# Layer 0's expert tiles and the scan's preparation rearranged: results leave from another queue, fetched rows are transposed behind a later tile, one logarithm for each preparation

## Chip, core and metric

The kernel runs on one core of one Trainium2 chip. The metric is device time in microseconds of one execution. Four runs of the kernel before gave 4164.61, 4164.91, 4173.64 and 4187.34, a median of 4169.28. One further execution was profiled.

## What is computed

Four images of 256 channels and 32 by 32 pixels go through two layers. All of it is float32.

- Layer 0, mixer: attention with 8 heads in which each row keeps only its largest scores, a 3 by 3 convolution of the values, a projection, and a residual.
- Layer 0, feed-forward: each of 4096 pixels is normalised and routed to 2 of 8 experts. An expert is `gelu(t @ w1 + b1) @ w2 + b2` with 256 hidden units, and the weighted sum and the residual give the pixel's new value.
- Layer 1, mixer: `x` is normalised, and a selective scan is run over the pixels in four directions. Its step size is `delta = softplus(xm @ W_delta + b_delta)`, and its input is `delta * xm` times a row of B.
- Layer 1, feed-forward: again 2 of 8 experts, with 1024 hidden units.

The part of the reference that matters here, shortened:

```python
out = tokens                                   # layer 0's feed-forward
for e in range(E):
    h = jax.nn.gelu(tokens @ w1[e] + b1[e], approximate=False)
    out = out + combine[:, e:e + 1] * (h @ w2[e] + b2[e])
...
delta = jax.nn.softplus(x @ W_delta + b_delta)  # layer 1's mixer
dBx = (delta * x)[..., None] * Bm[:, :, None, :]
y = jnp.einsum('blcn,bln->blc', h, Cm) + x * D
```

## The kernel before

The images stay in SBUF in the four tiles `x[b]`, channels on partitions, 1024 pixels in the free dimension (`L`), in two halves of 512 (`HALF`).

**Routing.** For each image, pixels are normalised (`norm`), routed (`route`) and scattered as rows into expert blocks in DRAM, `slots_x0` (lines 1487 to 1503). The blocks are then worked off in tiles of `T` = 256 rows. 36 tiles (`USUAL`) are always run; three more lie in a branch that this input does not take. The order of tiles has three phases, so that image 0's rows are all in the first 15 tiles (`FIRST`) and image 1's in the first 23 (`SECOND`).

**One tile** (`tile0`, lines 1507 to 1550). SyncE (SP) loads a block's rows `xs` (259 KB, 4 buffers), and the expert's `w1` and `w2` (256 KB each, 3 buffers). VectorE (DVE) picks the biases and the rows' weights. TensorE (PE) transposes the rows into `tp`, DVE copies them to `xe`, PE makes `hp`, ScalarE (ACT) applies Gelu to `hid`, PE makes `yp`, DVE and ACT add the bias and weigh it (`ys`, 4 buffers), and SP stores `ys` into `slots_y0` (line 1550).

**Beside the tiles.** `whole(b)` (line 1565) brings an image's rows back: 16 indirect DMAs on GpSimd (POOL) fetch rows of `slots_y0` into `y` (`fetched`, line 1451; the second eight add to the first eight), and `completed` (lines 1459 to 1468) transposes them on PE and adds them to `x[b]`. After image 0 comes `Prep(0).steps`, the preparation for the scan of image 0. In the loop over tiles (lines 1573 to 1578) four steps of each generator go ahead of a tile. With `times` = 2 and `pause(8)`, the transposes come four tiles after the first fetch in program order.

This part is not written as a fixed order. A scheduler at compile time orders each engine's instructions by its own model of their times, with program order as priority, so an instruction that the model takes for ready can go ahead of earlier code. On the chip each engine, and each engine's DMA queue, then works in that order: an instruction that has to wait holds up all behind it.

Every store into `slots_y0` and every fetch from it has an address known only at run time, so a fetch waits for all earlier stores, and a store for all earlier fetches.

**The preparation** (`Prep.steps`, line 1332) is run four times. `Prep(0)` is run beside layer 0's tiles, the other three inside the scan. After the normalisation it handles `zp`, the step size before softplus, in four parts, 2 channel tiles by 2 halves, each 128 by 512. In the version before, two parts form a group `c`:

```python
yield from begin(0)          # PE zp; ACT Relu, Abs, Exp
yield from begin(1)
lost(0); lost(1)             # six DVE operations together, line 1417
nc.scalar.activation(sp[:, 2:], sp[:, 2:], AF.Ln)          # line 1430, once per group
nc.vector.scalar_tensor_tensor(dd, sp[:, h], -0.5, dd, ALU.mult, ALU.add)  # 1434
nc.gpsimd.tensor_tensor(dd, dd, sp[:, 2 + h], ALU.add)     # line 1435
```

and `rest` (line 1390) then multiplies `dx = delta * xm` on POOL (line 1393) and updates `x` on DVE (line 1394).

**The scan** (lines 1715 to 1795) is 128 turns in an order written out by hand. A turn has on DVE the scans of lines 1671, 1680 and 1697 and two products (line 1707); on PE five groups of four matmul records of 512 columns; on POOL the product `uu` (line 1658), the product of line 1691 and a small difference; and on ACT three exponentials and a copy. Twice in each turn one step of the preparation of the next image is slipped in, once at the turn's beginning and once just ahead of the scan of line 1697. Images 2 and 3 are fetched and completed in the first 32 turns, and from the second image on the pixels of the image before are routed for layer 1.

Of the kernel before, what the change touches and what calls it, by code (L numbers as in the profile page):

```python
# [11 lines left out]
F32 = mybir.dt.float32  # L12
# [4 lines left out]
AF = mybir.ActivationFunctionType  # L17
# [44 lines left out]
def metaformer(ctx: ExitStack, tc: tile.TileContext, t: dict, out: bass.AP):  # L62
# [1259 lines left out]
    class Prep:  # L1322
# [9 lines left out]
        def steps(self, room, psum, tag):  # L1332
# [44 lines left out]
            bc = room("sp", [4 * HALF])[: 2 * NS, :L]  # L1377
# [12 lines left out]
            def rest(c):  # L1390
                for h in range(NHALF):
                    cols = ts(h, HALF)
                    nc.gpsimd.tensor_tensor(self.dx[:, c, cols], self.delta[:, c, cols], xm[:, c, cols], ALU.mult)
                    nc.vector.scalar_tensor_tensor(x[b][:, c, cols], xm[:, c, cols], dsk[:, c : c + 1],
                                                   x[b][:, c, cols], ALU.mult, ALU.add)
                    yield
                    yield

            behind = iter(())
            for c in range(CT):  # L1400
                sp = room("sp", [4 * HALF]).rearrange("p (k n) -> p k n", k=4)

                def begin(h):
                    cols = ts(h, HALF)
                    zp = psum.tile([P, HALF], F32, tag=tag, name="zp")
                    for k in range(CT):
                        nc.tensor.matmul(zp, wd[:, k, ts(c, P)], xm[:, k, cols],
                                         start=(k == 0), stop=(k == CT - 1))
                    next(behind, None)
                    yield  # L1410
                    nc.scalar.activation(self.delta[:, c, cols], zp, AF.Relu, bias=bd[:, c : c + 1])
                    nc.scalar.activation(sp[:, h], zp, AF.Abs, bias=bd[:, c : c + 1])
                    nc.scalar.activation(sp[:, h], sp[:, h], AF.Exp, scale=-1.0)
                    next(behind, None)
                    yield

                def lost(h):
                    v, up, dd = sp[:, h], sp[:, 2 + h], self.dx[:, c, ts(h, HALF)]
                    nc.vector.tensor_scalar(up, v, 1.0, None, ALU.add)
                    nc.vector.scalar_tensor_tensor(dd, up, 1.0, v, ALU.subtract, ALU.subtract, reverse1=True)  # L1420
                    nc.vector.scalar_tensor_tensor(v, v, 2.0, dd, ALU.subtract, ALU.mult)

                yield from begin(0)
                yield from begin(1)
                for _ in behind:
                    pass
                lost(0)
                lost(1)
                yield
                nc.scalar.activation(sp[:, 2:], sp[:, 2:], AF.Ln)  # L1430
                yield
                for h in range(NHALF):
                    dd = self.delta[:, c, ts(h, HALF)]
                    nc.vector.scalar_tensor_tensor(dd, sp[:, h], -0.5, dd, ALU.mult, ALU.add)
                    nc.gpsimd.tensor_tensor(dd, dd, sp[:, 2 + h], ALU.add)
                yield
                yield
                behind = rest(c)
            for _ in behind:
                yield  # L1440
            yield
            yield
# [15 lines left out]

    def completed(b, h, y, psum, tag):

        for c in range(CT):
            op = psum.tile([P, HALF], F32, tag=tag, name="op")
            for i in range(4):
                nc.tensor.transpose(op[:, ts(i, P)], y[:, i, ts(c, P)], ident)
            yield
            xs = x[b][:, c, ts(h, HALF)]
            nc.vector.tensor_tensor(xs, op, xs, ALU.add)
            yield
# [5 lines left out]
    with ExitStack() as st:  # L1474
        wp = st.enter_context(tc.tile_pool(name="m0_w", bufs=1))
        pb = st.enter_context(tc.tile_pool(name="m0_b", bufs=2))
# [3 lines left out]

        b1 = load(wp, "b1_0", [P, E, CT])
        b2 = wp.tile([P, E, C], F32, tag="b2_0", name="b2_0")
        nc.sync.dma_start(b2, t["b2_0"].rearrange("e d -> (e d)").partition_broadcast(P).rearrange(
            "p (e d) -> p e d", e=E))
        tokens = [wp.tile([P, NT, W0], F32, tag=f"tok{b}", name=f"tok{b}") for b in range(B)]
        scattered = nc.alloc_semaphore("scattered")
        for b in range(B):
            d = pb.tile([P, CT, L], F32, tag="d", name="d")
            here = slot0[:, :, ts(b, NT)]
            for _ in norm(b, 0, tokens[b], pb, ps_n, "t", "t", d):  # L1490
                pass
            for _ in route(b, 0, tokens[b], here, wp.tile([P, 2560], F32, tag="numbers", name="numbers"), ps_n, "t"):
                pass

            with tc.tile_critical(name=f"scatter{b}", no_gpsimd_drain=True):
                for n in range(NT):
                    for k in range(2):
                        nc.gpsimd.indirect_dma_start(
                            out=slots_x0, out_offset=bass.IndirectOffsetOnAxis(ap=here[:, k, n : n + 1], axis=0),
                            in_=tokens[b][:, n], in_offset=None).then_inc(scattered, 16)  # L1500
                nc.gpsimd.wait_ge(scattered, 16 * 2 * NT * (b + 1))
                if b == B - 1:
                    nc.clear_and_free_semaphores([scattered])

        blocks_x, blocks_y = (a.rearrange("(k a p) c -> k p a c", a=T // P, p=P) for a in (slots_x0, slots_y0))

        def tile0(i):
            def register(k, most, engines):
                return nc.values_load(every.which[0:1, k, i : i + 1], engines=engines, min_val=0, max_val=most,
                                      skip_runtime_bounds_check_because="the minimum with that of a count")  # L1510

            block = register(1, E * BLOCKS, [mybir.EngineType.SP])
            xs = pb.tile([P, T // P, W0], F32, tag="xs", name="xs", bufs=4)
            nc.sync.dma_start(xs, blocks_x[bass.ds(block, 1)].rearrange("o p a c -> p (o a) c"))
            e = register(0, E - 1, [mybir.EngineType.SP, mybir.EngineType.DVE])
            w1 = pb.tile([P, CT, C], F32, tag="w1", name="w1", bufs=3)
            nc.sync.dma_start(w1, t["w1_0"][bass.ds(e, 1)].rearrange("o (c p) f -> p (o c) f", p=P))
            w2 = pb.tile([P, CT, C], F32, tag="w2", name="w2", bufs=3)
            nc.sync.dma_start(w2, t["w2_0"][bass.ds(e, 1)].rearrange("o (c p) f -> p (o c) f", p=P))
            b1e = pb.tile([P, CT], F32, tag="b1e", name="b1e")  # L1520
            nc.vector.tensor_copy(b1e, b1[:, bass.ds(e, 1)].rearrange("p o c -> p (o c)"))
            b2e = pb.tile([P, C], F32, tag="b2e", name="b2e")
            nc.vector.tensor_copy(b2e, b2[:, bass.ds(e, 1)].rearrange("p o d -> p (o d)"))
            best = pb.tile([P, T // P], F32, tag="best", name="best")
            nc.vector.tensor_scalar(best, xs[:, :, C], every.expert[:, i : i + 1], None, ALU.is_equal)
            wt = pb.tile([P, T // P], F32, tag="wt", name="wt")
            nc.vector.tensor_tensor(wt, best, xs[:, :, C + 1], ALU.mult)
            nc.vector.tensor_tensor(wt, wt, xs[:, :, C + 2], ALU.add)
            tp = ps1.tile([P, CT, T], F32, tag="tp", name="tp")
            for a in range(T // P):  # L1530
                for c in range(CT):
                    nc.tensor.transpose(tp[:, c, ts(a, P)], xs[:, a, ts(c, P)], ident)
            xe = pb.tile([P, CT, T], F32, tag="xe", name="xe")
            nc.vector.tensor_copy(xe, tp)
            hp = ps_h.tile([P, CT, T], F32, tag="hp", name="hp")
            hid = pb.tile([P, CT, T], F32, tag="hid", name="hid")
            for f in range(CT):
                for c in range(CT):
                    nc.tensor.matmul(hp[:, f], w1[:, c, ts(f, P)], xe[:, c], start=(c == 0), stop=(c == CT - 1))
                nc.scalar.activation(hid[:, f], hp[:, f], AF.Gelu, bias=b1e[:, f : f + 1])  # L1540
            yp = ps1.tile([P, T // P, C], F32, tag="yp", name="yp")
            for a in range(T // P):
                for f in range(CT):
                    nc.tensor.matmul(yp[:, a], hid[:, f, ts(a, P)], w2[:, f, :], start=(f == 0), stop=(f == CT - 1))
# [468 lines left out]
```

## Time and profile before

| what | value |
|---|---|
| median of 4 runs | 4169.28 us |
| the profiled execution, its own time | 4186.96 us |
| its span, first to last instruction | 4185.2 us |
| attention, to the last projection | about 0 to 1925 us |
| routing of layer 0 | 1931 to 2072 us |
| layer 0's tiles, first transpose to last `yp` | 2074.7 to 2298.3 us |
| the scan with three preparations | 2302.8 to 3597 us |
| layer 1's tiles and the output | 3597 to 4185 us |
| busy in the scan (1294 us): PE, DVE, ACT, POOL | 1227, 1162, 885, 729 us |

The profiled execution lies at the upper end of the four runs, 17.7 us over their median; 1.8 us of its time lie outside its span. In the timeline a row gives start, duration, engine, line and operation, and in brackets how long the engine was idle before, and what ended that. "SPq" is the moment at which SP issues a DMA. PE records of one line are merged, and a fast record of 512 columns takes a quarter of 1.72 us.

### The profile page before, as it was taken

What the parts mean: (1) busy time and instruction counts of PE and PEld (TensorE: products, weight loads), DVE (VectorE), ACT (ScalarE), POOL (GpSimd) and SP (SyncE); (2) the same over time, 40 slices, a digit from 0 to 9 for tenths busy, and PEclk for the clock granted to TensorE, in tenths of its full rate; (3) what the DMA queues carried; (4) which work ended last, traced back from release to release, by engine and by line L of the source; (5) the groups of instructions that cost most, each with busy time, mean ns of one, the idle gap of its engine ahead of it and who ended that gap; (6) DMA issues with size and microseconds to landing.
All of it is one profiled execution on the core that took longest, in us unless ns stands there. A gap on an engine that the chain in (4) does not pass through costs nothing. (4 is left out here: it accounts for less than half of the span.)

```text
span 4185.2 us, 50303 instructions
## 1 busy us (share of the span) xinstructions
PE 3545.5 (85%) x17502; PEld 1966.5 (47%) x17502; DVE 3040.4 (73%) x5327; ACT 2847.3 (68%) x3823; POOL 1824.1 (44%) x1436
## 2 busy tenths in 40 slices
PE   8378878888888878965387899999999999999996
PEld 5144434444444434433265334443443434688885
DVE  2689898989898989893356889889899899411112
ACT  2889999999999999973235677767667677422222
POOL 0145444554455445552413666446446546221111
PEclk8568887788778877877699999999999999999997
DMA  9300093007200000001375433323333334555565
GB/s 285 93 1 1 1 246 93 1 1 262 73 1 1 11 1 1 11 1 35 104 207 154 129 109 131 105 100 113 116 97 120 115 102 135 178 186 189 186 193 185
DMA packets 280988, 426.40 MB, mean 102 GB/s; under 512 B 31889, under 2 KB 223634, under 8 KB 280594
## 3 DMA queue, kind: packets, MB, share of 16 engines
q1 hardware_dynamic: 259920, 382.66, 30.1%
q0 software_dynamic: 17024, 38.98, 3.0%
q8 instruction: 143, 2.34, 0.2%
q10 hardware_dynamic: 3778, 1.41, 0.1%
q14 instruction: 123, 1.01, 0.1%
HBM read 280.34 MB, written 142.64 MB: 101 GB/s over the span
## 5 line engine op out<-in xcount | busy, mean ns | idle before, releaser
L490 POOL TENSOR_SCALAR dr<-s_n,last 128x1024 bf16<-128x1024 f32 x256 | 732.3, 2878 | 877.0 <-DVE state L518 343.9
L406 ACT ACTIVATE junk_a<-s_n,state 128x1024 int8<-128x1024 f32 x448 | 514.7, 1149 | 28.0 <-DVE state L524 8.0
L1691 POOL TENSOR_TENSOR da_c<-prod,come 128x1024 f32<-128x1024 f32 x128 | 248.2, 1939 | 386.3 <-DVE h L1697 381.6
L410 DVE TENSOR_SCALAR_CACHE_REDUCE junk_v<-s_n,state 128x1024 int8<-128x1024 f32 x320 | 408.7, 1277 | 8.8
L1861 ACT ACTIVATE hid<-hp,b 128x256 f32<-128x256 f32 x288 | 133.7, 474 | 355.7 <-PE hp L1859 355.1
L457 DVE SCALAR_TENSOR_TENSOR w<-s_n,win 128x1024 f32<-128x1024 f32 x256 | 350.3, 1368 | 5.3
L460 DVE MAX8 win<-w 128x8 f32<-128x1024 f32 x256 | 314.5, 1228 | 8.9
L558 ACT ACTIVATE ex<-sT 128x1024 f32<-128x1024 f32 x256 | 247.1, 1015 | 100.5 <-PE sT L550 100.3
L1658 POOL TENSOR_TENSOR uu<-dx,bb 128x1024 f32<-128x1024 f32 x128 | 305.0, 2383 | 1.4 <-DMA bb<-bc_d 1.4
L1697 DVE TENSOR_TENSOR_SCAN h<-da_c,uu 128x1024 f32<-128x1024 f32 x128 | 302.8, 2365 | 0.0
L406 ACT ACTIVATE junk_a<-s_n,guess 128x1024 int8<-128x1024 f32 x256 | 294.2, 1149 | 7.4
L1671 DVE TENSOR_TENSOR_SCAN h<-da,uu 128x1024 f32<-128x1024 f32 x128 | 290.7, 2271 | 4.6 <-POOL uu L1658 4.6
L1680 DVE TENSOR_TENSOR_SCAN h<-da,uu 128x1024 f32<-128x1024 f32 x128 | 289.8, 2264 | 0.0
L568 PE MATMUL o_ps<-ex,vT 128*32 128x256 f32 x2048 | 244.2, 454 | 46.0 <-ACT ex L558 37.1
L1701 PE MATMUL hp<-h,ident 128*128 128x512 f32 x512 | 249.3, 610 | 31.1 <-DVE h L1697 30.5
L1645 ACT ACTIVATE da_c<-delta,a_log 128x1024 f32<-128x1024 f32 x128 | 268.4, 2097 | 0.2
L1859 PE MATMUL hp<-xe,w 128*128 128x256 f32 x1152 | 259.6, 382 | 6.1 <-DVE xe L1847 5.9
L440 ACT COPY s_n<-sp 128x1024 f32<-128x1024 f32 x256 | 245.6, 1004 | 25.3 <-POOL dr L490 12.8
L1666 PE MATMUL hp<-da_c,ident 128*128 128x512 f32 x512 | 246.4, 604 | 18.3 <-POOL da_c L1691 16.3
L1870 DVE TENSOR_TENSOR ys<-yp,b2e 128x512 f32<-128x512 f32 x36 | 24.9, 692 | 325.5 <-PE yp L1867 300.3
L1666 PE MATMUL hp<-h,twice 128*128 128x512 f32 x512 | 243.8, 599 | 17.7 <-issue 13.8
L1659 ACT COPY uu<-uu 128x1024 f32<-128x1024 f32 x128 | 253.6, 1981 | 3.8 <-POOL uu L1658 3.8
(542 smaller groups left out, 7564.2 us busy)
## 6 DMA issues: line engine op xcount, KB each, us to landing
bb<-bc_d SPq DMA_DIRECT2D x128, 512.0 KB
cb<-bc_d SPq DMA_DIRECT2D x128, 512.0 KB
w<-in_w SPq DMA_DIRECT2D x36, 1024.0 KB
w2e<-in_w SPq DMA_DIRECT2D x36, 1024.0 KB
slots_x<-zeros SPq DMA_DIRECT2D x1, 33411.0 KB
slots_x<-zeros SPq DMA_DIRECT2D x1, 33282.0 KB
slots_y<-zeros SPq DMA_DIRECT2D x1, 33024.0 KB
w<-in_w SPq DMA_DIRECT2D x72, 256.0 KB
```

The source lines that it names most:

```text
L406: nc.scalar.activation(junk, self.row(r), AF.Sign, bias=thr, scale=-1.0, accum_out=u)
L410: nc.vector.tensor_scalar(junk, self.row(r), thr, None, ALU.is_lt, ALU.add, accum_out=u)
L457: nc.vector.scalar_tensor_tensor(w, self.row(r), self.win[:, r, 0:1], self.row(r), ALU.is_gt if r < LAST_DVE else ALU.is_ge, ALU.subtract, ...
L460: nc.vector.max(out=self.win[:, r, 1:], in_=w)
L490: ins = nc.gpsimd.tensor_scalar(dr, self.row(r), self.last[:, r : r + 1], None, ALU.is_lt)
L1645: nc.scalar.activation(grid(self.da_c), cols_flipped(self.prep.delta[:, self.c]), AF.Exp, scale=self.decay)
L1658: nc.gpsimd.tensor_tensor(self.uu[:, 0], self.prep.dx[:, self.c], self.bb, ALU.mult)
L1666: nc.tensor.matmul(self.hp[h], ident if eye is None else eye, view[:, ts(h, HW // NHALF), :], start=first, stop=last)
L1671: nc.vector.tensor_tensor_scan(rows.rearrange("p r w -> p (r w)"), self.da, self.uu[:, 0], 0.0, ALU.mult, ALU.add)
L1680: nc.vector.tensor_tensor_scan(hs[:, ::-1], self.da[:, ::-1], self.uu[:, 0][:, ::-1], 0.0, ALU.mult, ALU.add)
L1697: nc.vector.tensor_tensor_scan(hs, self.da_c, self.uu[:, 1], 0.0, ALU.mult, ALU.add)
L1859: nc.tensor.matmul(hp[:, f % 2], self.w1[:, c, ts(f, P)], self.xe[:, c], start=(c == 0), stop=(c == CT - 1))
```

## The change

It is confined to `Prep.steps`, `completed` and the block of layer 0's feed-forward.

- A tile becomes a class with steps. The store into `slots_y0` is issued from POOL's queue; `xs` has 6 buffers, `w1` and `w2` 4, `ys` 8. The routing gets pools of its own, which are closed before the tiles' pools are opened.
- The steps beside the tiles come after a tile, four fetches are issued in a step, and the pause is 20 steps.
- The first transpose of each group of `completed` gets an edge to the last matmul of the tile before it in program order, so the scheduler can't put it earlier. It is an order on PE alone and no semaphore. In the scan the edge is not made.
- The preparation calculates one logarithm over all four parts, `Ln(v + 1)`, after the last of them. The correction for what `v + 1` loses is two DVE operations for each part, put one part behind. The additions and `dx` are on DVE; POOL has no part in them.

```diff
-                def lost(h):
-                    v, up, dd = sp[:, h], sp[:, 2 + h], self.dx[:, c, ts(h, HALF)]
-                    nc.vector.tensor_scalar(up, v, 1.0, None, ALU.add)
-                    nc.vector.scalar_tensor_tensor(dd, up, 1.0, v, ALU.subtract, ALU.subtract, reverse1=True)
-                    nc.vector.scalar_tensor_tensor(v, v, 2.0, dd, ALU.subtract, ALU.mult)
...
+            def lost(c, cols):
+                back = self.dx[:, c, cols]
+                nc.vector.tensor_scalar(back, v[:, c, cols], 1.0, 1.0, ALU.add, ALU.subtract)
+                nc.vector.tensor_tensor(back, v[:, c, cols], back, ALU.subtract)
+
+            for i, (c, cols) in enumerate(parts):
...
+                if i:
+                    lost(*parts[i - 1])
                 yield
...
+            lost(*parts[-1])
+            yield
+            nc.scalar.activation(v, v, AF.Ln, bias=1.0)
+            yield
+            for c, cols in parts:
+                dx = self.dx[:, c, cols]
+                nc.vector.tensor_tensor(dx, dx, v[:, c, cols], ALU.add)
+                nc.vector.tensor_tensor(self.delta[:, c, cols], self.delta[:, c, cols], dx, ALU.add)
                 yield
                 yield
+                nc.vector.tensor_tensor(dx, self.delta[:, c, cols], xm[:, c, cols], ALU.mult)
+                nc.vector.scalar_tensor_tensor(x[b][:, c, cols], xm[:, c, cols], dsk[:, c : c + 1],
+                                               x[b][:, c, cols], ALU.mult, ALU.add)
                 yield
+                yield
...
+    anchor = [None]
...
+                ins = nc.tensor.transpose(op[:, ts(i, P)], y[:, i, ts(c, P)], ident)
+                if i == 0 and anchor[0] is not None:
+                    tc.add_manual_dep(ins.ins, anchor[0].ins.name,
+                                      mybir.DependencyInfo(mybir.DependencyClass.NoSync,
+                                                           mybir.DependencyReason.DATA))
...
+            def store(self):
+                for a in range(T // P):
+                    nc.scalar.mul(self.ys[:, a], self.ys[:, a], self.wt[:, a : a + 1])
+                    nc.vector.scalar_tensor_tensor(self.ys[:, a], self.xs[:, a, :C], self.best[:, a : a + 1],
+                                                   self.ys[:, a], ALU.mult, ALU.add)
+                block = self.register(1, E * BLOCKS, [mybir.EngineType.Pool])
+                nc.gpsimd.dma_start(blocks_y[bass.ds(block, 1)].rearrange("o p a c -> p (o a) c"), self.ys)
...
-            yield from fetched(b, y, range(NHALF), 2)
-            yield from pause(8)
+            yield from fetched(b, y, range(NHALF), 4)
+            yield from pause(20)
...
         for i in range(USUAL):
+            one_tile = Tile0(i)
+            for step in ("load", "small", "turned", "hidden", "result", "store"):
+                getattr(one_tile, step)()
+            anchor[0] = one_tile.last
             for first_tile, steps in beside:
                 if i >= first_tile:
                     for _ in range(4):
                         next(steps, None)
-            tile0(i)
```

## The prediction

> **What bounds the kernel now.** I read the stages first (busy time by stretch), then the timelines of the two stages that the change touches, one engine at a time. The chain of waits reaches back only to 3587 us, so it does not judge them. In layer 0's tiles PE is the bound as long as nothing interrupts it: from tile to tile `ys` (line 1546) starts 4.34 us apart (2151.04, 2155.38), with PE 80.1 of 85.4 us busy up to 2160. Then this comes, in PE's timeline:
>
> ```profile
> 2169.11 1.06 PE L1539 MATMUL hp<-xe,w 128*128 128x256 f32 x2
> 2173.87 0.56 PE L1464 MATMUL op<-ident,y 128*128 128x128 f32 x2 [3.71 <-DMA y<-slots_y,slot]
> ...
> 2229.12 1.03 PE L1539 MATMUL hp<-xe,w 128*128 128x256 f32 x4
> 2233.37 0.33 PE L1464 MATMUL op<-ident,y 128*128 128x128 f32 x1 [3.22 <-DMA y<-slots_y,slot]
> ```
>
> PE, in order, stands at transposes of rows that have not been fetched, once for each image. And in SP's and POOL's timelines:
>
> ```profile
> 2157.82 0.37 SPq L1514 DMA_DIRECT2D xs<-slots_x  x1
> 2165.41 0.40 SPq L1550 DMA_DIRECT2D slots_y<-ys  x1
> ...
> 2228.88 0.37 SPq L1517 DMA_DIRECT2D w<-in_w  x1
> 2246.47 0.40 SPq L1550 DMA_DIRECT2D slots_y<-ys  x1
> ```
>
> ```profile
> 2162.28 0.95 POOL L1451 DMA_INDIRECT y<-slots_y,slot  x1 [0.30 <-issue]
> ...
> 2168.35 1.60 POOL L1451 DMA_INDIRECT y<-slots_y,slot  x1 [5.13 <-DMA slots_y<-ys]
> ```
>
> SP is silent for 7.6 and 17.6 us: a store waits for fetches, and the loads of the next tiles are queued behind it.
>
> In the scan a turn (from one start of line 1671 on DVE to the next) takes 7.87 us where DVE is the bound and 8.58 us where PE is; with a `zp` on PE it is 10.3 (1.72 more). DVE and POOL around the preparation:
>
> ```profile
> 2848.08 1.27 DVE L1434 SCALAR_TENSOR_TENSOR delta<-sp,delta 128x512 f32<-128x512 f32 x2
> 2848.90 4.79 POOL L1435 TENSOR_TENSOR delta<-delta,sp 128x512 f32<-128x512 f32 x2 [0.40 <-DVE delta L1434]
> 2849.26 3.37 DVE L1697 TENSOR_TENSOR_SCAN h<-da_c,uu 128x1024 f32<-128x1024 f32 x1
> ...
> 2859.09 3.64 DVE L1697 TENSOR_TENSOR_SCAN h<-da_c,uu 128x1024 f32<-128x1024 f32 x1
> 2859.30 1.28 POOL L1393 TENSOR_TENSOR dx<-delta,xm 128x512 f32<-128x512 f32 x1
> ```
>
> The scan of line 1697, 2.27 us elsewhere, takes 3.37 and 3.64 beside POOL's products. POOL's help costs DVE as much as it saves.
>
> **The tiles, step by step.** From the first transpose (2074.67) to the last `yp` (2298.25) 223.6 us pass. Tile 14's `yp` ends at 2146.7; the stage before that I leave as it is. Behind it lie 21 tiles x 4.34 = 91.1 us of PE, eight groups of fetched transposes x 0.43 = 3.5, and `Prep(0)`: mean 3.4, variance 3.4, `ln_rb` 1.8, `bp` 3.4, `zp` 6.9, together 18.9 (records at full clock in the scan: 1.72 for four of 512 columns, 1.70 for 16 variance records). That is 113.5 us, so 2260.2 without a stall; 38 us are lost now. What stays lost:
>
> - *First fetch.* It comes behind tile 15's store. `yp` ends at 2151.0; 2.4 to the store (2146.7 to 2149.13), 4.1 to the fetch (2149.13 to 2153.22), 0.5 for POOL's issue (line 1941, the same 256 KB, 0.54 us). First fetch at 2158.0; eight x 1.26, the gap of 5.1, eight x 1.84 give 2187.9; 2.4 to landing. The first half's rows are in at 2183.0, the second's at 2190.3. The first half's transposes stand behind tile 21 (2177.0): a wait of 6, then 0.9 of them and a tile, and 2 more. **8 us.** Four fetches a step and the pause of 20 do that; without the edge the scheduler would put them early, as now.
> - *Second fetch.* From tile 23's end 7.0 + 10.1 + 5.1 + 14.7 + 2.4 = 39.3 us. Until tile 29's end PE has 26.0 of tiles and 18.9 of preparation, 44.9. **0**, with that work as its cover; were the preparation's matmuls done earlier, 13.
> - *POOL's power (line 1359)* lies in program order behind the second image's 16 fetches (before, ahead of them). If the scheduler puts it ahead of them it costs 0; behind eight, the 10.1 us of their issue come late against the 6 that PE has before `ln_rb`: 4 to 5; behind all 16, about 29. I take **3**.
> - *ACT.* Each part needs Relu, Abs, Exp (about 1.8) and two table loads of 1.28; 12 loads now become about 10. Three tiles with four parts and the logarithm (2.1 + 2.6) make about 27 us of ACT against 22 of PE. With the waits for Gelu **8**; bounds 4 (PE's loss from 2252.6 to 2272.9, four tiles: 3) and 14.
> - *Last tile,* 3.1 idle ahead of 2293.83 behind table loads: unchanged, **3**.
>
> The sum: 2260.2 + 22 = 2282 against 2298: **16 us less**; bounds 0 and 34. The store's queue: 36 x 0.54 us on a POOL that is idle from 2069.9 to 2153; register loads and the wait come on top, and 4.3 us a tile are there for them. Behind the waiting store on POOL stand only later stores, fetches and the power; eight `ys` hold eight tiles, 35 us, as long as the fetches' 32. SP's order loses the waiting store, and six `xs` let loads run ahead.
>
> A rule against this: the Trainium skill, "DMA: Bandwidth & Descriptors", section "Issuing engines are not separate DMA queues", says that issuing from several engines saves only the sequencer's issue time. By it alone the move would be worth an estimated 36 x 0.4 us of SP, which is idle, so nothing; the rows show why it isn't the whole: what is saved is a wait in SP's order, 7.6 and 17.6 us. "SBUF — State Buffer", section "SBUF: two separate sides", says that VectorE's fast copies keep GpSimd from writing descriptors. The row nearest to that, the fetches of 0.95 us beside `b2e` copies of 0.29, shows no such hold.
>
> **The preparation in the scan, three times.** DVE's work for a part goes from 0.34 + 3 x 0.60 + 0.65 = 2.8 us (net of overlap, lines 1419, 1420, 1421, 1434, 1394) to 0.34 + 4 x 0.60 + 0.65 = 3.4. No float32 `tensor_tensor` with both inputs in SBUF is in the trace at this size; bounds are 0.34 (line 1419) and 0.65 (line 1394), and I take 0.60, as the two-input rows beside it. So DVE gets 2.4 us more for each preparation; POOL loses 4 x (2.4 + 1.28) us. For the second preparation, 13 turns from 2811.0 to 2939.5 take 128.5 us now: among them 13.9 and 11.8 (six `lost` operations in one turn, 3.6 us; PE idle behind them) and five of 10.1 to 10.3 in which line 1697 or 1686 is stretched by POOL. After: a `lost` of 0.95 falls in each `zp` turn, where DVE has 10.3 - 7.87 = 2.4 to spare, and then eight turns have 1.2 more on DVE. 7.9 + 10.6 + 3 x 10.3 + 8 x 9.1 = 122.2: **6 us less**. The third likewise (the same turns, 128.6). The first, with fetches and completions beside it, has the same two heavy turns (14.5, 11.9) and more stretched ones: **9**. The logarithm of 2048 columns with its loads is 4.7 us of ACT in one turn, which has some 3 idle; its results are used a turn later, so 0, or 2 if that slack is not there. Sum **22 us less**; bounds 8 and 32.
>
> **Together** 38 us: 4186.96 - 38 = 4149 for the profiled execution. The median lies 17.7 lower; the four runs spread by 0.5%, with the profiled one at their upper end, and I carry the difference over: 4169.3 - 38 = **4131**.
>
> **Rivals.**
> 1. *The power or the fetches still hold PE.* The power behind all 16 fetches adds 26 us, and the tiles gain nothing: 4169 - 22 + 10 = 4157; with the edge useless, 4147. For it: program order. Against: POOL waits for tile 23's store, then 5.1 us between the two eights, and the power is ready about then.
> 2. *The scan gains nothing* because PE is the bound in those turns. Then only the tiles' 16 count: 4153. For it: PE 1227 of 1294 us busy, DVE 1162. Against: PE's idle of 1.5 us behind the heavy turns (line 1701 waits for line 1697).
> 3. *Slower.* The moved DVE operations read two SBUF tensors, as line 1697 does; if POOL's `uu` or line 1691 runs beside them, each is held by 1.4 us (3.64 against 2.27). 3 x 16 such operations x 1.4 = 67 us: 4169 - 16 - 22 + 67 = 4198. It outweighs the gain once 27 of the 48 are hit. Against: between line 1686 and 1697, where they stand, POOL has finished `uu` (2910.0 against 2910.5) and only issues an indirect DMA.
> 4. *Neither part does what it says* (waits only change place): 4169.
>
> **Numbers.** The forecast has 0.60 (4131, or somewhat less where fetches are faster); rival 1 0.17, half of it still faster by over 0.5%; rival 2 0.10; rival 3 0.06; rival 4 0.07. 0.5%, 21 us, is about what a measurement of this kernel can tell from no change. Faster 0.60 + 0.09 = 0.69, rounded up to 0.70 for the case between rivals 1 and 2; same 0.24; slower 0.06. The range: with both gains at their best 34 + 32, 4103; a little inside that, and up to rivals 1 and 2: 4108 to 4158.
>
> **What would show it.** In the tiles' stage: SP without silences of over 5 us; line 1464 waiting some 8 us for the first image and under 3 for the second; the last `yp` some 16 us sooner after the first transpose. If line 1371 or 1363 waits for line 1359, rival 1 is at work. In the scan: no turn over 11 us in the `zp` part, line 1697 at 2.27 throughout, the scan some 22 us shorter. If `tensor_tensor` rows of the preparation last over 1.2 us, rival 3. The prediction is wrong if PE's loss behind ACT's table loads grows past 14 us, or if the stores land so late from POOL's queue that the transposes wait over 20 us.

## The result and the profile after

The changed kernel takes 4165.28 us (median of 52 runs) against 4173.05 us for the kernel before (78 runs taken with them): a ratio of **0.9985, 95% interval 0.9975 to 0.9994**. By the ratio that is some 6 us less, by the medians 7.8, where 38 were forecast. The time lies above the range on record (4108 to 4158).

The stages, read off the timelines, in us. The columns are the profile before, the profile after, a second profile of the changed kernel (the run `after_again` below), and the best kernel of the experiments (`stores_lag_again`).

| stage | before | after | after, 2nd | best |
|---|---|---|---|---|
| start to the end of attention | 1924.2 | 1902.4 | 1910.5 | 1905.2 |
| to layer 0's first transpose | 150.5 | 155.9 | 139.0 | 137.7 |
| **tiles**: first transpose to last `yp` | **223.6** | **238.7** | **231.9** | **196.7** |
| to the first scan | 11.4 | 12.9 | 13.7 | 19.9 |
| **scan**: first start to last end | **1275.6** | **1259.5** | **1258.6** | **1258.8** |
| to the end of the span | 599.9 | 596.5 | 596.0 | 596.8 |

The two profiled spans differ by 19.3 us (4185.2 and 4165.9), but attention, which the change doesn't touch, differs by 21.8: spans can't be compared here, stages can. The scan got 16 us shorter, of a forecast 22. The tiles got 8 to 15 us longer instead of 16 shorter.

Lines have moved: 1464 is now 1447, 1550 is 1564, 1697 is 1717, 1671 is 1691, 1686 is 1706; 1359 to 1364 have stayed. What the change was made for did happen. The transposes of fetched rows on TensorE, in the timeline of the changed kernel:

```profile
2168.79 1.04 PE L1447 MATMUL op<-ident,y 128*128 128x128 f32 x8
2174.13 1.04 PE L1447 MATMUL op<-ident,y 128*128 128x128 f32 x8
```

No bracket follows: they waited for nothing, where before they came in pieces with waits of 3.71, 3.22 and more. In the second profile the first of them waits 2.40 us; in this one a stand of three engines, told below, had held the tiles back by some 9 us, so that the rows had more time. But TensorE, VectorE and POOL have this a little later, each in its own timeline:

```profile
2200.28 0.59 PE L1553 MATMUL yp<-w,hid 128*128 128x256 f32 x2
2232.64 1.22 PE L1545 MATMUL hp<-xe,w 128*128 128x256 f32 x2 [31.77 <-DVE xe L1525]
```

```profile
2198.29 0.69 DVE L1556 TENSOR_TENSOR ys<-yp,b2e 128x512 f32<-128x512 f32 x1 [0.94 <-PE yp L1553]
2231.50 0.17 DVE L1361 TENSOR_TENSOR ln_rr<-ln_r 128x8 f32<-128x8 f32 x1 [32.51 <-POOL ln_r L1359]
...
2231.90 0.68 DVE L1525 COPY xe<-tp 128x512 f32<-128x512 f32 x1
```

```profile
2205.15 1.02 POOL L1432 DMA_INDIRECT y<-slots_y,slot  x1 [3.62 <-DMA slots_y<-ys]
...
2228.21 1.54 POOL L1432 DMA_INDIRECT y<-slots_y,slot  x1 [0.30 <-issue]
2229.20 2.27 POOL L1359 TENSOR_TENSOR ln_r<-ln_ve,power 128x8 f32<-128x8 f32 x1
```

Read them from the last to the first. POOL's power (line 1359) stands behind the second image's 16 fetches. VectorE, in order, stands at line 1361 for the power; behind it in VectorE's order stands the copy `xe` (line 1525) of the next tile, and TensorE waits for that copy. One small product of 128 x 8 holds VectorE and TensorE for 32 us, and ScalarE, which gets nothing from them, stands for 37.43 (line 1560). Rival 1 had this case, at a chance of 0.17. In the kernel before, the power stood ahead of these fetches, and VectorE waited 1.63 us for it (POOL, then VectorE):

```profile
2198.24 1.69 POOL L1359 TENSOR_TENSOR ln_r<-ln_ve,power 128x8 f32<-128x8 f32 x1 [15.35 <-DVE ln_ve L1356]
2213.27 1.49 POOL L1451 DMA_INDIRECT y<-slots_y,slot  x1 [13.35 <-PE hp L1539]
```

```profile
2199.96 0.17 DVE L1361 TENSOR_TENSOR ln_rr<-ln_r 128x8 f32<-128x8 f32 x1 [1.63 <-POOL ln_r L1359]
```

In the scan, VectorE in a turn of the second preparation:

```profile
2871.98 0.21 DVE L1706 TENSOR_TENSOR_SCAN come<-prod,gap 128x32 f32<-128x32 f32 x1
2872.11 0.67 DVE L1419 TENSOR_TENSOR dx<-delta,xm 128x512 f32<-128x512 f32 x1
2872.69 0.75 DVE L1420 SCALAR_TENSOR_TENSOR x<-xm,dskip,x 128x512 f32<-128x512 f32 x1
2873.35 2.29 DVE L1717 TENSOR_TENSOR_SCAN h<-da_c,uu 128x1024 f32<-128x1024 f32 x1
```

The moved product takes 0.67 us (0.60 net was taken, bounds 0.34 and 0.65), and line 1717 keeps its 2.29, where beside POOL's products it had 3.37 and 3.64. Rival 3 is out. In the first preparation's heaviest turn VectorE now has this (the turn ends at 2439.74, 14.23 us after its start):

```profile
2439.14 0.69 DVE L1454 TENSOR_TENSOR x<-op,x 128x512 f32<-128x512 f32 x1 [3.23 <-PE op L1447]
```

### The profile page after: what moved, and what is told of

Same layout as the page of the kernel before. It is cut to its first block, busy times and chain, and to the rows that moved or that the text cites. A ratio compares the mean times of both kernels' runs of the same rounds, so it can differ in the third digit from the quotient of the medians.

```text
span 4165.9 us, 50283 instructions
## 1 busy us (share of the span) xinstructions
PE 3520.8 (85%) x17502; PEld 1953.3 (47%) x17502; DVE 3025.0 (73%) x5343; ACT 2832.1 (68%) x3809; POOL 1789.5 (43%) x1440
## 5 line engine op out<-in xcount | busy, mean ns | idle before, releaser
L1717 DVE TENSOR_TENSOR_SCAN h<-da_c,uu 128x1024 f32<-128x1024 f32 x128 | 291.0, 2274 | 0.0
L1887 PE MATMUL yp<-w2e,hid 128*128 128x256 f32 x1152 | 255.9, 379 | 0.0
```

Source lines behind the costliest of these rows:

```text
L1717: nc.vector.tensor_tensor_scan(hs, self.da_c, self.uu[:, 1], 0.0, ALU.mult, ALU.add)
L1887: nc.tensor.matmul(yp[:, a], self.hid[:, f, ts(a, P)], self.w2[:, f, :], start=(f == 0), stop=(f == NF - 1))
```

## The experiments

Theory A: the power stands behind the fetches in POOL's order. Rivals: the fetches themselves hold the other engines (B), or the wait would only change place (C). All stages in one table (us; the ratio is against the kernel before run beside it on the same chip). "To scan" is the time from the last `yp` to the first scan, 11.4 in the kernel before: what a run gains in the tiles it can lose again there. Each stage is read from one profile.

| run | tiles | to scan | scan | ratio, 95% interval |
|---|---|---|---|---|
| `power_first` | 211.2 | 13.8 | 1260.7 | 0.9936 (0.9911 to 0.9961) |
| `tiles_only` | 233.1 | 12.9 | 1277.4 | 1.0014 (0.9994 to 1.0034) |
| `prep_only` | 224.3 | 11.0 | 1260.5 | 0.9953 (0.9931 to 0.9974) |
| `pf_no_edge` | 212.4 | 17.6 | 1258.7 | 0.9934 (0.9914 to 0.9955) |
| `stores_lag` | 206.6 | 14.4 | 1260.7 | 0.9915 (0.9892 to 0.9939) |
| `pf_sp_store` | 224.8 | 12.0 | 1258.5 | 0.9946 (0.9926 to 0.9966) |
| `pf_few_bufs` | 217.2 | 17.4 | 1260.6 | 0.9946 (0.9923 to 0.9968) |
| `pf_dx_pool` | 216.1 | 13.7 | 1271.9 | one run |
| `after_again` | 231.9 | 13.7 | 1258.6 | 0.9970 (0.9950 to 0.9990) |
| `stores_lag_again` | 196.7 | 19.9 | 1258.8 | 0.9928 (0.9905 to 0.9951) |
| `lag_short_pause` | 214.9 | 13.0 | 1258.7 | one run |
| `lag_short_no_edge` | 229.8 | 13.4 | 1259.6 | one run |

**The power ahead of the fetches** (`power_first`).

```diff
-        beside = [(FIRST, chain(whole(0), preps[0].steps(room, ps_n, "t"))), (SECOND, whole(1))]
+        beside = [(FIRST, chain(whole(0), preps[0].steps(room, ps_n, "t"))), (SECOND + 1, whole(1))]
```

> The changed kernel, with the second image's fetches beginning one tile later, so that POOL's power (line 1359) stands ahead of them in POOL's order. In the changed kernel VectorE waits 32.51 us at line 1361 and TensorE 31.77 us behind it; the stage from the first transpose to the last yp takes 238.7 us. Theory A (POOL's order: the power stood behind 16 fetches): the wait at line 1361 shrinks below 4 us, TensorE's long gap goes, the stage takes 200 to 208 us, the whole about 33 us less than the changed kernel, so some 39 us below the kernel before (ratio about 0.991). Theory B (the fetches themselves hold VectorE or TensorE while POOL issues them): a gap of over 20 us stays while the second image's fetches are issued, under another line's name; stage over 225 us. Theory C (the wait only changes place): line 1447 waits 15 us or more for the second image's rows, which are fetched a tile later; stage 215 to 225 us.

The stage fell by 27.5 us against the first profile after, and by 20.7 against the second; the ratio is 0.9936, where about 0.991 was expected. No gap lies beside the second fetches, so B is out for this stall; the transposes wait 3.5 us in all, so C is out. But line 1361 still waits 13.94 us, and the stage is 3 us above what was expected. POOL's timeline shows what is left:

```profile
2154.32 0.78 POOL L1564 DMA_DIRECT2D slots_y<-ys  x1 [3.76 <-issue]
...
2175.01 0.72 POOL L1564 DMA_DIRECT2D slots_y<-ys  x1 [2.43 <-DMA slots_y<-ys]
2178.18 0.71 POOL L1564 DMA_DIRECT2D slots_y<-ys  x1 [2.44 <-DMA slots_y<-ys]
2178.90 1.70 POOL L1359 TENSOR_TENSOR ln_r<-ln_ve,power 128x8 f32<-128x8 f32 x1
```

The first image's fetches hold POOL for 25 us; the stores pile up behind them. Each store then waits until the one before has landed (2.43 us of idleness at the least, "DMA slots_y<-ys"; 2.5 to 3.7 us from issue to landing), so they follow one another at 3.13 to 4.30 us, and eight of them stand ahead of the power, whose input was ready at 2166.69.

**Each part alone** (`tiles_only`, `prep_only`): the preparation's code of one kernel put into the other.

> The tiles of the changed kernel with the preparation of the kernel before: the scan should run as before the change. Theory A: the power stands behind the second image's fetches here too, so the tiles' stage is again some 15 us (or a few more: two more table loads of 1.28 us) longer than the 223.6 us of the kernel before, and the scan is unchanged turn by turn (second preparation's turns 128.6 us); the whole is about 15 us slower than before, ratio about 1.004. Rival (the new preparation, not the tiles, lengthens the tiles' stage): stage at or below 215 us, ratio below 1.

> The preparation of the changed kernel with the tiles of the kernel before. If the preparation's gain in the scan is its own: turns with zp 10.3 us and those after it 9.1 to 9.2 us, the second and third preparation about 6 us shorter each, the first about 4; the scan 14 to 17 us shorter than before; the tiles' stage within 5 us of 223.6 us; ratio about 0.996. Rival (the scan's gain needs the new tiles' stage, or is a matter of the clock): scan shorter by under 5 us, ratio above 0.999.

Both as expected, with a smaller loss for the tiles alone: 9.5 us longer, not 15 or more, and a ratio of 1.0014 (1.004 expected) whose interval holds 1. VectorE's waits in `tiles_only` name the same line:

```profile
DVE ln_rr L1361 <- POOL ln_r L1359: 33.5, 1, 33.5
```

So the stall belongs to the tiles' part, with either preparation; the preparation alone gains 15 us in the scan, whatever stands before it. Its ratio of 0.9953 is the whole gain of the change, and the tiles gave some of it back.

**Without the edge** (`pf_no_edge`): the power ahead, and this line left out, so that no transpose is tied to a tile.

```diff
-            anchor[0] = one_tile.last
```

> As the run with the power ahead, but without the edge that ties the transposes of fetched rows behind a later tile's last matmul: the scheduler may put them early again. If the edge carries the gain (as was forecast): line 1447 waits for fetched rows about 10 us in the first image and 10 in the second, the stage is 15 to 25 us longer than with the edge. If the pause of 20 steps and the deeper buffers alone do it: stage within 4 us of the run with the edge.

The stage is 1.2 us longer and the ratios are alike, so most of what the edge was forecast to do the pause of 20 steps does. That the edge is worth nothing beside it isn't shown: without the edge line 1447 waits 8.7 us for the first image (3.5 in all with it), a part of which goes unseen because VectorE then waits 12.21 us for the power instead of 13.94, and the first scan comes 17.6 us behind the last `yp` instead of 13.8.

**The stores behind the power** (`stores_lag`): `finish` is the arithmetic of `store`, which keeps the register load and the DMA.

```diff
+        stores, LAG = [], 5
...
+            stores.append(one_tile)
+            while len(stores) > (LAG if FIRST < i <= SECOND + 1 else 0):
+                stores.pop(0).store()
...
+                    while i == first_tile > FIRST and stores:
+                        tied = stores.pop(0).store()
+                        tc.add_manual_dep(tied.ins, preps[0].powered.ins.name, ...)
```

> As the run with the power ahead of the second fetches, but from tile 16 on a store is issued five tiles behind its tile, and those still out when the second image's fetches are due are tied behind the power: it now has 4 stores ahead of it on POOL instead of 8. In the run with the power ahead, eight stores stood at 3.15 to 4.3 us from one to the next behind the first image's fetches (2154.32 to 2178.18), the power came at 2178.90, and VectorE waited 13.94 us for it. Theory A2 (what is left of the loss is the stores that were put on POOL, which catch up slowly after the fetches): the wait at line 1361 falls below 4 us, TensorE's gap of 11.8 us goes, the stage takes 196 to 202 us against 211.2, and the whole about 12 us less. Rival (the stores' lag only moves the backlog: transposes of the second image or ys buffers wait instead): stage above 207 us.

The first profile had 206.6, above the 196 to 202 expected and just below the rival's 207, with 1.87 us of wait at line 1361. In it three engines stood with no releaser in the records (the brackets say `issue` or `remote` and name no instruction), as in the first profile of the changed kernel, where it looks like this (TensorE, then ScalarE):

```profile
2156.23 2.08 PE L1545 MATMUL hp<-xe,w 128*128 128x256 f32 x4 [4.35 <-issue]
```

```profile
2155.70 0.47 ACT L1547 ACTIVATE hid<-hp,b1e 128x256 f32<-128x256 f32 x1 [6.33 <-remote]
2160.73 0.47 ACT L1547 ACTIVATE hid<-hp,b1e 128x256 f32<-128x256 f32 x1 [3.77 <-remote]
```

It comes some 5 us after the first fetches begin. Both kernels were profiled again to see whose it is.

> The changed kernel once more, for a second profile. In its first one TensorE, VectorE and ScalarE stood for 3 to 6 us each at about 2150 to 2160 us, with no releaser in the records, while the first image's fetches ran; its first transpose of fetched rows came 110.5 us after the stage's first transpose, against 100.5 in the run with the power ahead. If that is a matter of the execution: first transpose of fetched rows at 100 to 104 us in this profile, stage 228 to 232 us. If it belongs to the kernel: 110 again, stage 238. The wait of 32 us at line 1361 stays in both.

> The run with the lagged stores once more. Its first profile had the same unexplained stand (stage 206.6 us where 196 to 202 was expected). If that is a matter of the execution: stage 196 to 201 us now; if it belongs to the kernel: 205 to 208. The whole 0.8 to 1.0% below the kernel before.

It is a matter of the execution: 231.9 and 196.7 us now, and the first transpose of fetched rows comes 101.1 and 100.5 us into the stage, against 110.5 and 108.4. The stage of 196.7 lies inside what theory A2 expected. POOL and VectorE in that profile (lines are 2 further on):

```profile
2164.32 0.71 POOL L1566 DMA_DIRECT2D slots_y<-ys  x1 [3.11 <-DMA slots_y<-ys]
2165.85 1.69 POOL L1359 TENSOR_TENSOR ln_r<-ln_ve,power 128x8 f32<-128x8 f32 x1 [0.82 <-DVE ln_ve L1356]
```

```profile
2167.57 0.17 DVE L1361 TENSOR_TENSOR ln_rr<-ln_r 128x8 f32<-128x8 f32 x1 [1.87 <-POOL ln_r L1359]
```

The power now waits for its input, not for POOL. Against 231.9 that is 35 us, and 14.5 against `power_first`. A part comes back at the end of the stage: POOL still issues stores up to 2250.33, 11 us behind the last `yp`, and the operation with which the scan begins waits for them:

```profile
2253.08 2.29 DVE L1819 TENSOR_TENSOR_SCAN cum<-inner,delta 128x1024 f32<-128x1024 f32 x1 [9.99 <-DMA slots_y<-ys]
```

The time from the last `yp` to the first scan is 19.9 us, against 13.7 (`after_again`) and 13.8 (`power_first`), so up to the first scan the gains are 29 and 8.4 us. In this much the rival, by which the lag only moves the backlog, was right. The ratios are 0.9915 and 0.9928: less than the kernel before and than the changed kernel (0.9985 and 0.9970), while the interval overlaps that of `power_first` (0.9936).

**The queue of the stores** (`pf_sp_store`): the power ahead, results from SP's queue.

```diff
-                block = self.register(1, E * BLOCKS, [mybir.EngineType.Pool])
-                nc.gpsimd.dma_start(
+                block = self.register(1, E * BLOCKS, [mybir.EngineType.SP])
+                nc.sync.dma_start(
```

> As the run with the power ahead, with the results stored from SP's queue again, as before the change. Theory A2: POOL has nothing ahead of the power but the first fetches, so line 1361 waits under 4 us and the 11.8 us of TensorE go; SP stands silent behind waiting stores again (two silences of 8 to 18 us), and with six xs and four w1, w2 that costs 0 to 8 us: stage 199 to 207 us against 211.2. Rival (the move to POOL's queue is what gained, as was forecast): SP's silences starve TensorE as before the change; waits for xs or w of over 15 us; stage above 215 us.

My expectation fell and the rival's stage held; TensorE's waits for `xs` are 14.3 us, just under its 15. SP's timeline, then TensorE's:

```profile
2129.79 0.01 SPq L1517 DMA_DIRECT2D w<-in_w  x1
2152.86 0.40 SPq L1564 DMA_DIRECT2D slots_y<-ys  x1
```

```profile
2156.77 1.09 PE L1523 MATMUL tp<-ident,xs 128*128 128x128 f32 x4 [10.31 <-DMA xs<-slots_x]
```

SP is silent for 23 us behind a waiting store, and six `xs` don't cover it. Nothing but the first fetches stands ahead of the power there (line 1361 waits 1.87 us), and still the stage is 13.6 us longer than in `power_first`, and 28 longer than in `stores_lag_again`. Of the 13.6 us, 5.0 are lost by the end of tile 14, before the first fetch; the rows don't show by which wait. The move of the stores gained by itself; what it cost is `power_first`'s 13.94 us, eight stores ahead of the power. The rule that the prediction took from the Trainium skill, "DMA: Bandwidth & Descriptors", section "Issuing engines are not separate DMA queues", speaks of issue time alone, and by that the move would have been worth nothing.

**The buffers** (`pf_few_bufs`): the power ahead, with 4 `xs`, 3 `w1` and `w2`, 4 `ys`.

```diff
-                self.ys = pb.tile([P, T // P, C], F32, tag="ys", name="ys", bufs=8)
+                self.ys = pb.tile([P, T // P, C], F32, tag="ys", name="ys", bufs=4)
```

> As the run with the power ahead, with the buffers of the kernel before (4 xs, 3 of w1 and w2, 4 ys). POOL is taken up by 16 fetches for 25 us and by stores at 3.15 us after that; eight ys hold 35 us of tiles, four hold 17. If the deeper ys carry that: line 1556 waits for a free ys twice, some 8 to 15 us each time, and the stage is 15 to 25 us longer than 211.2. If the buffers do nothing: within 3 us of 211.

The wait is there, in VectorE's list (us in total, times, longest):

```profile
DVE ys L1556 <- DMA slots_y<-ys: 14.9, 2, 11.4
```

The two waits are 11.4 and 3.6 us, where 8 to 15 each were expected. The stage is only 6.0 us longer, below the 15 to 25 expected: line 1361 waits 1.88 us here instead of 13.94. With four `ys` the tiles stand for the stores first, and by the time the power's input is ready the stores ahead of it are issued; the one wait took the place of the other. Against `stores_lag_again`, which has neither, it is 20.5 us.

**The pause and the edge** (`lag_short_pause`, `lag_short_no_edge`), on the kernel with the lagged stores.

```diff
-            yield from fetched(b, y, range(NHALF), 4)
-            yield from pause(20)
+            yield from fetched(b, y, range(NHALF), 2)
+            yield from pause(8)
...
+            yield from pause(8)
```

> As the run with the lagged stores, with the times of the kernel before: two fetches a step and a pause of 8 (8 steps more behind the transposes, so that the preparation stays where it is); the edge stays. The transposes of fetched rows stand two tiles (8.7 us) sooner. If the pause carried the gain: line 1447 waits 5 to 10 us in all for each image, stage 10 to 20 us longer. If the edge carries it: no wait over 3 us, stage within 4 us.

> As the run with the short pause, and without the edge: the transposes stand spread over the tiles before, the first of them a tile sooner still. If the edge is worth anything, it is here: line 1447 waits in several pieces, 10 us or more for an image, and the stage is 4 to 10 us longer than with the edge and the short pause. If it is worth nothing: within 3 us of that run.

TensorE's waits at line 1447, first with the edge, then without:

```profile
PE op L1447 <- DMA y<-slots_y,slot: 19.4, 9, 5.8
```

```profile
PE op L1447 <- DMA y<-slots_y,slot: 32.0, 9, 14.2
```

The short pause costs 18.2 us (214.9 against 196.7; 11.2 up to the first scan), and there the edge is worth 14.9, more than the 4 to 10 expected. So the pause carried most of the gain of the transposes, and the edge is of clear use where the pause is too short. Both are single runs with one profile each.

**POOL's product again** (`pf_dx_pool`): the power ahead, and the product of delta and xm back on POOL.

```diff
-                nc.vector.tensor_tensor(dx, self.delta[:, c, cols], xm[:, c, cols], ALU.mult)
+                nc.gpsimd.tensor_tensor(dx, self.delta[:, c, cols], xm[:, c, cols], ALU.mult)
```

> As the run with the power ahead, with the product of delta and xm (four a preparation) back on POOL. Theory (POOL's product beside a scan stretches the scan of line 1717 from 2.27 to about 3.6 us, so that POOL's help costs what it saves or more): the four turns of a preparation that hold it go from 9.12 us to 9.5 to 10.2, a preparation gets 1.5 to 4 us longer. Rival (the product on VectorE is the whole of the 9.12 against 7.87): those turns fall to 8.5 us or less and each preparation is 2 to 3 us shorter.

The second preparation's four turns take 10.43, 10.27, 10.27 and 10.26 us where VectorE's own product gave 9.14, 9.12, 9.12 and 9.12: 4.7 us more for this preparation, more than the 1.5 to 4 expected, and the scan is 11 us longer. But it isn't line 1717 that is stretched, as the theory had it (2.29 at the most in this run); it is line 1706. VectorE, then POOL:

```profile
2829.21 2.09 DVE L1706 TENSOR_TENSOR_SCAN come<-prod,gap 128x32 f32<-128x32 f32 x1
2831.23 0.72 DVE L1420 SCALAR_TENSOR_TENSOR x<-xm,dskip,x 128x512 f32<-128x512 f32 x1
```

```profile
2829.93 1.28 POOL L1419 TENSOR_TENSOR dx<-delta,xm 128x512 f32<-128x512 f32 x1
```

Line 1706, a scan of 128 x 32 that takes 0.21 elsewhere, ends at 2831.30, as POOL's product ends (2831.21). To save 0.67 us VectorE pays 1.9. The Trainium skill, "SBUF — State Buffer", section "Who interferes with whom", says that a VectorE instruction with two inputs in SBUF contends with a GpSimd instruction that reads SBUF, and that the shared ports are an exclusive lock. The two ends agree with that; the starts don't tell who held what, for the scan starts 0.72 us ahead of the product. The price is the 1.9 us measured here.

## Why the prediction was wrong, by its steps

- **POOL's power: the step that failed.** It was put at 3 us, between 0 (ahead of the fetches) and 29 (behind all 16); it cost 31.8 on TensorE, 32.5 and 32.8 in the two profiles on VectorE. The upper end was worked out rightly and given too little weight. The argument against it, that POOL has a gap of 5.1 us between the two eights, failed as well: all 16 fetches now come behind one tile, and in the changed kernel the eights follow each other at 0.30 us. And the price was looked for at `ln_rb` on TensorE ("6 that PE has before `ln_rb`"), while it is VectorE's line 1361 that waits, with the `xe` copies behind it. How the power came to stand there can be read off the steps: fetches and pause take 4 + 20 of them ahead of the preparation where they took 8 + 8, so at four a tile the preparation begins two tiles later. By this reading the power fell behind the second image's fetches; no run changes the steps alone, but one tile's delay of these fetches (`power_first`) put it ahead again.
- **The store's queue.** "36 x 0.54 us on a POOL that is idle" took the wait to be covered by the 4.3 us of a tile. It is, one store at a time: a store waits for the landing of the one before, some 3.15 us from one to the next. But behind 25 us of fetches that leaves 1.2 us of 4.34 a tile for catching up. This is what kept 11.8 us lost in `power_first`.
- **First fetch** 8 us: 0 and 2.4 in the two profiles, the 0 with the help of the stand. Without the gap between the eights the rows were nearly in time.
- **ACT** 8 us: TensorE's waits for `hid` behind tile 14 are 8.0 and 8.3 in the changed kernel, 9.3 with the lagged stores. **Last tile** 3: 0.6. **Second fetch** 0: 0.
- **The tiles in sum.** 2260.2 without a stall is a stage of 185.5 us. With the measured terms of the best kernel, 185.5 + 9.3 (ACT) + 3.2 (all waits at line 1447) = 198.0, and its stage is 196.7. With 32.1 for the power, 2.4 for the fetches and 8.3 for ACT, as in its second profile, the changed kernel comes to 228.3, measured 231.9; TensorE's busy time behind tile 14, forecast at 113.5 us, was 113.1 in the best kernel and 116.1 here. The frame of the sum held; one term was off by 29.
- **The scan.** 22 us were forecast and 16.1 came. The second preparation's 13 turns were forecast at 122.2 and took 122.9 (128.6 before), the third's 122.8; with the turn behind them (10.76 to 10.04) these two gave 6.4 and 6.5 of a forecast 6 each. The first gave 3.2 instead of 9 (turns 9 to 21, counted from 0: 139.1 to 135.9), and that is the whole shortfall: its heavy turn of 14.46 is still 14.23, because VectorE now waits 3.23 us there for line 1447 on TensorE, which stands behind `y` and `zp`; I had taken the six `lost` operations for the cause because they stood there. The logarithm cost nothing.
- **Rival 2** (the scan gains nothing) is out. **Rival 1** is what happened: its time was 12 us below the median of before, and 6 (0.9985) and 12 (0.9970) were measured.

What the stand of three engines beside the first fetches is stays open; its 8 to 10 us appear in three of the seven profiles in which nothing else delays that place (the first of the changed kernel, `stores_lag`, `pf_dx_pool`; the stage of the last isn't compared for that). ScalarE has waits named `remote` in `pf_sp_store` and `pf_few_bufs` too (7.5 and 3.9 us). There the waits for `xs` and `ys` that follow end with what comes behind the fetches, so the stand should not add to these stages; no second profile shows it.

## What to carry to other kernels

When work is moved to another engine's queue, or steps are put later in it, write down what is already in that queue and who waits for each of it, one step further than the direct reader: here a product of 128 x 8 took a place behind 16 fetches, and an in-order VectorE passed its wait on to TensorE. A queue that looks idle in the mean can be taken for 25 us at a stretch, and a chain of stores to one DRAM tensor catches up at the pace of its landings, not of its issue. Where a sum has a term with far ends and one side depends on an order that a scheduler chooses, neither the middle nor the kinder end is an estimate: make it two cases.

## What the runs showed of the hardware

- Stores from POOL's queue that depend on one another through one DRAM tensor follow at about 3.15 us (0.71 of issue, 2.43 of waiting) for 256 KB each where nothing else delays them, with a landing of 2.5 us; in `power_first` they took 3.13 to 4.30. The Trainium skill, "DMA: Bandwidth & Descriptors", section "Two DMAs through the same engine are not ordered", says that the issuing engine itself has to wait for the earlier DMA's semaphore; the rows show what that costs an engine that has other work in the same order.
- A fetch on POOL takes about 0.95 us to issue in the first eight, which write, and about 1.54 in the second eight, which add.
- After its stand of 32 us TensorE's next two matmuls take 1.22 us where two take 0.59: the granted clock is 0.89 in the 10 us ahead of the stand (2190 to 2200), 0.50 from 2232 to 2234, and 0.74 from 2233 to 2240.
